# The row of dinv: by way of DRAM instead of by transposes, and the additions of the first graph's outputs one step later, in a two-layer graph kernel

## The chip, the cores and the metric

The kernel runs on one core of a Trainium2 chip, in float32 throughout. The metric is the device time of one launch in microseconds (us); lower is better. The kernel before took 2661.98 us (median of 3 runs, 2660.5 to 2662.49). The profile is of a run of 2660.45 us, and its span from the first to the last instruction is 2658.7 us. Times below that are positions ("at 176.8 us") count from the start of that span.

Engines are named as in the profile: PE is the matrix engine, DVE the vector engine, ACT the scalar engine, POOL the engine that here does the small powers, some additions and issues many of the transfers, SP the one that issues the other transfers. Each engine runs its own instructions in the order in which the program emits them, and waits where an operand or a buffer isn't ready.

## What is computed

There are 16 graphs b of 1024 nodes with 256 features, and one 1024 x 1024 adjacency matrix for all.

```python
# layer 0, for each graph
h = relu(layernorm(x))
g = relu((h.T @ (adj * A_s(h))) * para)         # A_s: from column means of h
q, (k, v) = g.T, h @ kv_w                       # 4 heads of 64
x = x + softmax(q @ k.T * scale) @ v
# layer 1
h = relu(layernorm(x))
A_norm = adj + eye
deg = A_norm.sum(0) + A_norm.sum(1) - diagonal(A_norm)
dinv = rsqrt(deg)
A_hat = A_norm * dinv[:, None] * dinv[None, :]
agg = A_hat @ h
x = x + batchnorm(relu(batchnorm(agg @ W1.T)) @ W2.T)
```

dinv is one vector of 1024 numbers for all graphs. It is used twice: as a factor of each node's row (in the layernorm's scale), and as a factor of each output node of the aggregation. The aggregation is held transposed, with nodes along the columns, so there the kernel needs dinv along the columns, the same in all 128 partitions.

## The kernel before

Node t*128+p lies in partition p. A vector over nodes is a tile of 128 partitions x 8 columns; so is dinv, the last of six such vectors in the tile `deg_sm` (the profile writes `deg`). The row form is the tile `dbc` (128 x 1024; the profile writes `dbc_f`).

**Order.** The program fixes the order of the instructions on each engine by hand (`tc.manual_schedule()`); nothing is moved later. `attention()` (L956) runs over 16 steps for each graph: a *unit* is half of the features and half of the query nodes of a graph, and each of a graph's 4 units has 4 steps. In step s it emits, in this order: the scores of step s on PE with their exponentials on ACT (`scores`, L850, tiles `sc` and `p`), `finish()` of a unit that is due (4 transposes of its output on PE, L934), the first instruction of a piece of background work that asked to be put there (see below), `add_output()` of the unit that was finished (L942 to L952: DVE divides by the sums and adds to x), the sums of exponentials on DVE (`acc`, L885 and L888), the product with the values of step s-1 on PE (`o`, L899), if that was a unit's last step its `sums()` (L916 to L924), and then background work until the step's share of it is done.

**A unit's end.** `sums()` adds the exponentials over the partitions with PE, copies the result to the tile `row` on ACT (L918), and lets POOL send it to DRAM (`sums_d`, L919) and fetch it back across the partitions as `inv` (L924, twice). `add_output()` needs `inv`. A unit that ends in the step s of its `sums()` is put on `pending` with the step s + 2 (L998), and its `finish()` and `add_output()` come in that step.

**Background.** While graph b is in the attention, `background(b)` (L756) prepares graph b+1 or b+2 and, from b = 1 on, does the second layer's aggregation and first product of graph b-1. It is a generator. Each yield gives a cost; the total for a graph is spread over the 16 steps. A yield of `TOP` stops the background for the step, and what follows it is emitted near the top of the next step, before that step's value product.

For b = 0 the background is: queries of graph 1 (`plain_queries`), woven with `graph()` (L230), which forms seven combinations of blocks of the transposed adjacency on POOL and writes them to DRAM (`aht_d`), in 8 pieces of 4 subtractions, 2 loads and 3 stores; and with `degrees()` (L211), which reads the transposed adjacency (tiles `at`), sums it, and ends with dinv. The last step of dinv is `rsqrt` (L79), two POOL instructions (L81, L82). All of `graph()` stands ahead of it in POOL's order. Then come `load_later()` (L276), which loads W1 and allocates `dbc`; a product of keys and values; `columns_of(dinv)` (L183), two DVE copies that spread dinv to two tiles `cb_deg`; another product; and, after a `TOP`, `broadcast_row` (L194): 8 transposes on PE (`cbp_deg`, L199) and 2 copies on ACT to `dbc` (L200). Last comes `prepare(2, products)` (L738), which makes the same kind of row for graph 2 from `csum`: `cb_c` by `columns_of`, then `cbp_c`.

`dbc` is first read in the aggregation of graph 0, in the second graph's attention (L641).

**Buffers that matter.** W1 and `dbc` take the space that `graph()` uses for its adjacency tiles. The pool `py` with the tag `y` has 4 buffers, taken in turn by `two` and `one` of `graph()` (L260, L261; one of each for each piece), by `row` of each unit (L917), and by the `cb` tiles (L187). A new tile waits until the transfer out of the buffer's last tile has landed. The PSUM pool with the tag `mm` has 2 buffers, taken in turn by all products of the background; a product waits until the result two before it has been read. PSUM for the scores has 2 buffers, so that the scores of a step wait for the exponentials of the step before.

Of the kernel before, what the change touches and what calls it, by code (L numbers as in the profile page):

```python
# [10 lines left out]
F32 = mybir.dt.float32  # L11
# [6 lines left out]
P = 128  # L18
# [5 lines left out]
def gnn_two_layers_kernel(  # L24
# [12 lines left out]
    nc = tc.nc  # L37
    B, N, C = x.shape
# [30 lines left out]
    aht_d = dram.tile([7, NP // 2, P, TH, FB], F32, name="aht_d")  # L69
    y1_d = [dram.tile([P, HC, FB], F32, name=f"y1_d{i}") for i in range(B * NH)]  # L70

    sums_d = [dram.tile([2, FB], F32, name=f"sums_d{u}") for u in range(B * CC * NH)]

    UNITS = B * CC * NH
# [9 lines left out]
    def layers(shifted):  # L84
# [60 lines left out]
        def double(slots):  # L145

            for _ in slots:
                next(slots, None)
                yield 0.0
# [58 lines left out]
        later = {}  # L208
# [67 lines left out]
        def load_later():  # L276
            later["w1"] = big.tile([P, CC, H1], F32, tag="w1", name="w1")
            nc.sync.dma_start(out=later["w1"], in_=w1_t.rearrange("(k p) j -> p k j", p=P))
            later["dbc"] = const.tile([P, N], F32, tag="dbc", name=f"dbc_{kind}")

        class Norm:

# [83 lines left out]
        TOP = -1.0  # L366
# [389 lines left out]
        def background(b):  # L756

            if b == 0:
                differences_1 = columns_of(csums[1], "c1")
                yield TOP  # L760
                differences(1, differences_1)
                yield 1.0
                for k in range(CC):
                    yield TOP
                    transposed(1, k)
                    yield 1.0
                w, products, norm = weighers[1], keys_values(1), Norm(2, True).all()
                yield from weave(
                    islice(products, 4), (0, double(islice(w, 8))), (0, islice(norm, 4))
                )  # L770
                yield from weave(
                    plain_queries(1), (0, norm), (0, w), (5, graph()), (7, degrees())
                )
                load_later()
                yield from islice(products, 1)
                cbs = columns_of(dinv, "deg")
                yield from islice(products, 1)
                yield TOP
                broadcast_row(later["dbc"], cbs, "deg")
                yield 1.0  # L780
                yield from prepare(2, products)
                return
            before = hidden(b - 1)
            gather = aggregate(b - 1)
            if b + 1 < B:
                w, products, norm = weighers[b + 1], keys_values(b + 1), normed(b - 1)
                yield from weave(islice(products, 4), (0, islice(w, 4)))
                yield from weave(queries(b + 1), (0, double(w)), (9, islice(norm, 5)))
                yield next(gather)
                yield from weave(products, (0, norm))  # L790
            else:
                yield from weave(endings.pop(), (2, normed(b - 1)))
                yield next(gather)
            if b + 2 < B:
                yield from weave(gather, (7, Norm(b + 2, True).all()))
                yield from prepare(b + 2, before)
            elif b + 2 == B:

                yield from gather
                endings.append(before)  # L800
            else:
                yield from gather
                yield from weave(before, (0, normed_last()))
# [152 lines left out]
        def attention():  # L956

            units = [Unit(b, k, f) for b in range(B) for k in range(CC) for f in range(NH)]
            steps = [(u, g) for u in units for g in range(NG)]
            per_graph = CC * NH * NG  # L960
            before = None
            pending = []
            bg, done, total, top = iter(()), 0.0, 0.0, False
            for s in range(len(steps) + 2):
                if s < len(steps):
                    unit, g = steps[s]
                    b = unit.at[0]
                    if s % per_graph == 0:
                        run(bg)
                        top = False  # L970
                        bg, done = background(b), 0.0
                        total = (37.6 if b > 0 else 41.0) * (b + 1 < B) + 24.0 * (b > 0) + 6.0 * (b + 2 < B)
                        total += 13.7 * (0 < b < B - 2) + 27.4 * (b == B - 1) + 3.0 * (b == 0)

                        total -= 10.3 * (b == B - 1)
                    made = scores(*unit.at, g)
                    due = total * (s % per_graph + 1) / per_graph
                else:
                    due += 5.1
                ended = None  # L980
                if pending and pending[0][1] <= s:
                    ended = pending.pop(0)[0]
                    ended.finish()
                if top:
                    done += advance(bg)
                    top = False
                if ended is not None:
                    ended.add_output()
                if s < len(steps):
                    for pr in made:  # L990
                        unit.add(pr)
                if before is not None:
                    (last, g_last), prs = before
                    last.values(g_last, prs)
                    if g_last == NG - 1:
                        last.sums()

                        pending.append((last, s + (2 if last.index < UNITS - 2 else 1)))  # L998
                while done < due and not top:
                    cost = advance(bg)  # L1000
                    if cost is None:
                        break
                    if cost == TOP:
                        top = True
                        break
                    done += cost
                before = (steps[s], made) if s < len(steps) else None
            run(bg)

        with st:  # L1010
            if shifted:
                for b in range(B):
                    if b > 0:
                        load_x(b)
                    run(Norm(b, True).all())
                    differences(b, columns_of(csums[b], f"c{b}"))
                    for k in range(CC):
                        transposed(b, k)
                    run(islice(weighers[b], AHEAD))
                    run(weave(plain_queries(b), (0, weighers[b])))  # L1020
                    if b == 0:
                        run(degrees(), graph())
                        load_later()
                        broadcast_row(later["dbc"], columns_of(dinv, "deg"), "deg")
                    run(keys_values(b))
                    shifted_attention(b)
                    norm = Norm(b, False)
                    run(norm.all())
                    nc.gpsimd.dma_start(out=x1_d[b], in_=xs[b])
                    if b == B - 1:  # L1030
                        attn.close()
                        turns.append(second(kind))
                    run(aggregate(b), hidden(b))
            else:
                norm = Norm(0, True)
                norm.stats(0, 1)
                norm.scale(0, 2)
                for t in range(2, NT, 2):
                    norm.stats(t, t + 1)
                    norm.shift(t - 2, 2)  # L1040
                    norm.relu(t - 2, t - 1)
                    norm.scale(t, 2)
                norm.shift(NT - 2, 2)
                norm.relu(NT - 2, NT - 1)
                products = keys_values(0)

                for k in range(CC):
                    transposed(0, k, (0,))
                run(islice(products, 2))
                for k in range(CC):  # L1050
                    transposed(0, k, (1,))
                differences(0, columns_of(csums[0], "c0"))
                run(weave(products, (0, islice(weighers[0], AHEAD))))
                load_x(1)
                load_x(2)
                run(weave(plain_queries(0), (0, weighers[0]), (5, Norm(1, True).all())))
                attention()
                attn.close()
                turns.append(second(kind))
                run(aggregate(B - 1), hidden(B - 1))  # L1060
# [324 lines left out]
```

## Time and profile of the kernel before

| Engine | busy, us | share of the span | instructions |
|---|---|---|---|
| PE (matmul) | 2572.0 | 97% | 11882 |
| DVE | 1743.4 | 66% | 2768 |
| ACT | 1336.5 | 50% | 1937 |
| POOL | 564.0 | 21% | 648 |

Transfers moved 355.59 MB, 134 GB/s over the span. The mean granted PE clock was 0.988 of full speed.

Shares over the span say little on a change that touches two of sixteen graphs. The attention of graph 0 lies at about 60 to 206 us, that of graph 1 follows. Views that are read below: the waits of PE (who waited for whom, in us, how often, the longest), the busy time of each engine by stretches of the span, and the timeline (start, duration, engine, line, output <- input, number of instructions merged in the line, and in brackets how long the engine had idled and what ended it). In the timeline DMA_DIRECT2D is the issue of a transfer, not its time.

### The profile page before, as it was taken

The numbers are of one execution on the slowest core, as the hardware profiler recorded it, in microseconds if no ns is written. First come the engines' busy times: TensorE is split into PE (matmuls) and PEld (weight loads), VectorE is DVE, ScalarE is ACT, GpSimd is POOL, SyncE is SP. The second block draws the span as 40 slices with busy tenths as digits, with TensorE's granted clock in tenths as the row PEclk, the third lists the DMA queues.
The fourth block names the chain that finished last, engine by engine and source line by source line (L and its number), as shares of the span: only waits on it lengthen the run. The fifth ranks groups of instructions, "written<-read, shape, count | busy, mean of one in ns | idle before, by whom it ended". The sixth has DMA issues, their size and how long they took to land. (4 is left out here: it accounts for less than half of the span.)

```text
span 2658.7 us, 32181 instructions
## 1 busy us (share of the span) xinstructions
PE 2572.0 (97%) x11882; PEld 951.8 (36%) x11882; DVE 1743.4 (66%) x2768; ACT 1336.5 (50%) x1937; POOL 564.0 (21%) x648
## 2 busy tenths in 40 slices
PE   8959999999999999999999999999999999999995
PEld 3323333333333333333333333333333333334443
DVE  5537576666767675767666676757676675557675
ACT  5635463636454554546373645545463634335544
POOL 1461111111111111111111111111101111026653
PEclk9989999999999999999999999999999999999997
DMA  4451424242423324242424233231524232455559
GB/s 159 145 181 61 166 80 171 84 171 80 143 92 117 122 68 158 68 171 84 171 80 156 87 131 103 93 139 60 174 80 171 80 124 99 135 198 198 198 181 374
DMA packets 131686, 355.59 MB, mean 134 GB/s; under 512 B 17984, under 2 KB 34880, under 8 KB 125376
## 3 DMA queue, kind: packets, MB, share of 16 engines
q1 hardware_dynamic: 104768, 274.25, 29.4%
q0 software_dynamic: 26752, 79.20, 9.0%
q8 instruction: 96, 1.57, 0.2%
q14 instruction: 70, 0.57, 0.1%
HBM read 278.67 MB, written 74.71 MB: 133 GB/s over the span
## 5 line engine op out<-in xcount | busy, mean ns | idle before, releaser
L866 ACT ACTIVATE p<-sc 128x1024 f32<-128x1024 f32 x512 | 495.5, 1019 | 606.3 <-PE sc L858 605.2
L888 DVE TENSOR_TENSOR acc<-acc,p 128x1024 f32<-128x1024 f32 x384 | 471.7, 1228 | 132.0 <-ACT p L866 111.5
L858 PE MATMUL sc<-q,k 64*128 64x512 f32 x2048 | 508.8, 615 | 0.5 <-ACT p L866 0.5
L899 PE MATMUL o<-p,v 128*64 128x512 f32 x2048 | 496.7, 606 | 0.0
L158 PE MATMUL pg<-w,h_a 128*64 128x512 f32 x1600 | 358.1, 592 | 3.4 <-ACT k L595 1.7
L158 PE MATMUL pa<-aht,h_b 128*64 128x512 f32 x1536 | 343.5, 592 | 0.0
L858 PEld LDWEIGHTS sc<-q,k 64*128 64x128 f32 x2048 | 176.1, 186 | 320.4 <-issue 296.8
L919 POOL DMA_DIRECT2D sums_d<-row x64 | 37.5, 586 | 1032.0 <-ACT row L918 1032.0
L158 PE MATMUL py<-at,w 128*64 128x512 f32 x1024 | 230.4, 592 | 0.0
L899 PEld LDWEIGHTS o<-p,v 128*64 128x64 f32 x2048 | 124.5, 136 | 285.4 <-issue 284.7
L408 DVE SCALAR_TENSOR_TENSOR w<-w,adj 128x1024 f32<-128x1024 f32 x128 | 157.2, 1228 | 102.9 <-ACT w L429 99.1
L158 PEld LDWEIGHTS pg<-w,h_a 128*64 128x64 f32 x1600 | 115.5, 137 | 231.8 <-issue 212.8
L158 PEld LDWEIGHTS pa<-aht,h_b 128*64 128x64 f32 x1536 | 110.4, 137 | 213.3 <-issue 197.6
L708 ACT ACTIVATE y<-py,vec 128x512 f32<-128x512 f32 x128 | 87.6, 684 | 168.2 <-PE py L158 111.4
L421 ACT ACTIVATE w<-cbc,csum 128x512 f32<-128x512 f32 x256 | 170.0, 715 | 0.0
L885 DVE TENSOR_TENSOR acc<-p,p 128x1024 f32<-128x1024 f32 x64 | 78.4, 1226 | 109.5 <-ACT p L866 109.5
L709 POOL DMA_DIRECT2D y_d<-y x128 | 70.0, 547 | 316.7 <-ACT y L708 315.6
L429 ACT ACTIVATE w<-w 128x1024 f32<-128x1024 f32 x128 | 134.9, 1054 | 1.8
L483 DVE TENSOR_TENSOR w<-w,w 128x1024 f32<-128x1024 f32 x112 | 132.8, 1216 | 1.8 <-DVE w L408 0.5
L158 PE MATMUL pv<-kvw_f,ht 128*64 128x256 f32 x1024 | 121.0, 384 | 8.8 <-DVE q L575 5.2
L924 POOL DMA_DIRECT2D inv<-sums_d x128 | 98.2, 771 | 145.8 <-DMA sums_d<-row 109.6
L158 PEld LDWEIGHTS py<-at,w 128*64 128x64 f32 x1024 | 74.2, 137 | 145.2 <-issue 128.7
(155 smaller groups left out, 2868.8 us busy)
## 6 DMA issues: line engine op xcount, KB each, us to landing
aht<-aht_d SPq DMA_DIRECT2D x224, 512.0 KB, 6.2
adj<-in_adj_dram SPq DMA_DIRECT2D x128, 512.0 KB, 4.3
y_d<-y POOLq DMA_DIRECT2D x128, 256.0 KB, 2.6
yin_f<-y_d SPq DMA_DIRECT2D x32, 1024.0 KB, 6.3
x<-in_x_dram SPq DMA_DIRECT2D x32, 512.0 KB, 5.0
para<-in_para_dram SPq DMA_DIRECT2D x64, 256.0 KB, 3.9
x_d<-x POOLq DMA_DIRECT2D x16, 1024.0 KB, 10.3
xo_f<-x_d SPq DMA_DIRECT2D x32, 512.0 KB, 8.3
```

The source lines that it names most:

```text
L158: nc.tensor.matmul(dst[r], left[:, r], right, start=start, stop=stop)
L408: nc.vector.scalar_tensor_tensor(w, w, 1.0, a, op0=ALU.add, op1=ALU.mult)
L421: nc.scalar.activation(w[:, t, :], cbc[:, q * FB : (q + 1) * FB], AF.Abs, bias=csum[:, th * TH + t : th * TH + t + 1], scale=-1.0,)
L429: nc.scalar.activation(made[i], made[i], AF.Tanh, scale=-0.5 / C)
L483: nc.vector.tensor_sub(block(i)[part], block(x)[part], block(y)[part])
L708: nc.scalar.activation(y, made, AF.Identity, bias=b1[:, j : j + 1])
L858: nc.tensor.matmul(sc[:, e, :], ks[b][k][r, m * P : (m + 1) * P], qs[b][k][r, f * FB : (f + 1) * FB], start=True, stop=True,)
L866: nc.scalar.activation(pr, sc, AF.Exp)
L885: nc.vector.tensor_add(self.acc, self.held, pr)
L888: nc.vector.tensor_add(self.acc, self.acc, pr)
L899: nc.tensor.matmul(self.o[r, :], vs[b][k][:, m, r], pr[:, e, :], start=(m == 0), stop=(m == NT - 1),)
L924: nc.gpsimd.dma_start(out=self.inv[:, :, e], in_=sums_d[u][e].rearrange("(j q) -> q j", q=P))
```

## The change

dinv no longer goes to `dbc` by DVE copies, PE transposes and ACT copies in the background of graph 0. Instead `load_later()` writes dinv to a DRAM vector of 1024 numbers and reads it back to all partitions, both issued by SP. `load_later()`, the load of W1 with it, moves from the background of graph 0 to that of graph 1, behind the first four products and ahead of the queries of graph 2. This takes the wait for dinv out of DVE's and PE's order.

Separately, the units of graph 0 are finished three steps behind their `sums()` instead of two. This gives the way of the sums through DRAM one more step while POOL is busy with `graph()`.

```diff
+    dinv_d = dram.tile([N], F32, name="dinv_d")
...
             later["dbc"] = const.tile([P, N], F32, tag="dbc", name=f"dbc_{kind}")
+            nc.sync.dma_start(out=dinv_d.rearrange("(t p) -> p t", p=P), in_=dinv)
+            nc.sync.dma_start(
+                out=later["dbc"], in_=dinv_d.rearrange("(o n) -> o n", o=1).to_broadcast([P, N])
+            )
...
-                load_later()
-                yield from islice(products, 1)
-                cbs = columns_of(dinv, "deg")
-                yield from islice(products, 1)
-                yield TOP
-                broadcast_row(later["dbc"], cbs, "deg")
-                yield 1.0
+                yield from islice(products, 2)
                 yield from prepare(2, products)
                 return
...
                 yield from weave(islice(products, 4), (0, islice(w, 4)))
+                if b == 1:
+                    load_later()
                 yield from weave(queries(b + 1), (0, double(w)), (9, islice(norm, 5)))
...
-                        pending.append((last, s + (2 if last.index < UNITS - 2 else 1)))
+
+                        later_by = 3 if last.at[0] == 0 else 2
+                        pending.append((last, s + (later_by if last.index < UNITS - 2 else 1)))
```

A second form of the program, for inputs on which the softmax without a maximum would overflow (L1021 on), gets the same `load_later()`; it isn't run on these inputs.

More of the change, by code (lines that the diff above doesn't have):

```diff
@@ L1023, in layers @@
                         load_later()
-                        broadcast_row(later["dbc"], columns_of(dinv, "deg"), "deg")
                     run(keys_values(b))
```

## The prediction

> **What bounds the kernel now.** I read by stretches first, since 97% for PE hides where the other 3% lie. In each line: the stretch, then busy time of PE, PEld, DVE, ACT, POOL, the granted PE clock, the busy share of the transfer engines, GB/s.
>
> ```profile
> 86.00:163.00 77.00, 70.98 (x326) 24.18 (x326) 44.37 (x67) 49.14 (x78) 51.51 (x64) 0.98 0.59 202
> 163.00:192.00 29.00, 7.39 (x32) 3.38 (x32) 4.55 (x8) 3.60 (x5) 21.06 (x31) 0.65 0.60 204
> 192.00:290.00 98.00, 97.81 (x498) 37.28 (x496) 70.52 (x108) 53.78 (x73) 11.66 (x14) 1.00 0.35 119
> ```
>
> In the last line, the attention that follows, PE is idle for 0.2 us in all, so time is saved only where PE waits. From 163 to 192 it works 7.39 of 29 us. The waits of PE name the cause.
>
> ```profile
> PE cbp_deg L199 <- DVE cb_deg L188: 18.0, 1, 18.0
> ...
> PE pv L158 <- DVE q L575: 5.2, 1, 5.2
> ...
> PE cbp_deg L199 <- DVE v L612: 3.6, 1, 3.6
> ```
>
> Two of these three belong to the transposes that are removed, 21.6 us in sum. That is a ceiling for this part, not its worth: the timeline has to tell what else was late in those us.
>
> ```profile
> 162.97 1.99 PE L858 MATMUL sc<-q,k 64*128 64x512 f32 x8
> ...
> 173.33 0.71 POOL L272 DMA_DIRECT2D aht_d<-two  x1
> ...
> 175.79 0.38 SPq L278 DMA_DIRECT2D w<-in_w_t_dram  x1
> 176.27 1.47 SPq L170 DMA_DIRECT2D adj<-in_adj_dram  x3
> 176.77 0.59 ACT L918 COPY row<-sums 128x512 f32<-128x512 f32 x1 [15.68 <-DMA aht_d<-two]
> 177.25 1.95 ACT L866 ACTIVATE p<-sc 128x1024 f32<-128x1024 f32 x2
> ...
> 179.06 0.71 POOL L272 DMA_DIRECT2D aht_d<-two  x1
> ...
> 180.74 1.67 POOL L82 TENSOR_TENSOR deg<-deg,neg_half 128x8 f32<-128x8 f32 x1
> 182.39 0.64 POOL L919 DMA_DIRECT2D sums_d<-row  x1
> 182.45 0.43 DVE L188 COPY cb_deg<-deg 128x512 f32<-128x512 f32 x1 [21.41 <-POOL deg L82]
> ...
> 186.44 0.43 DVE L188 COPY cb_deg<-deg 128x512 f32<-128x512 f32 x1 [3.57 <-DMA aht_d<-two]
> ...
> 187.68 1.09 PE L199 MATMUL cbp_deg<-ident,cb_deg 128*128 128x128 f32 x4 [3.63 <-DVE v L612]
> 188.70 2.84 PE L899 MATMUL o<-p,v 128*64 128x512 f32 x8
> ...
> 193.19 1.99 PE L858 MATMUL sc<-q,k 64*128 64x512 f32 x8
> ```
>
> Here 162.97 is step 13 of graph 0, 193.19 step 14. Three things are late, all for POOL's sake. (1) ACT has the copy to `row` of the third unit at its head for 15.68 us, with the exponentials of step 13 behind it: `row` takes the buffer of `two` of the last piece but one, issued at 173.33 and landed at 176.77. (2) dinv's power ends at 182.4, behind the last piece of `graph()`. (3) The second `cb_deg` takes the buffer of the last `two`, issued at 179.06 and landed at 186.4: 7.4 us, against 3.4 for the one before. The change removes (2), and (1) and (3) stay.
>
> **What the Trainium skill says.** "DMA: Bandwidth & Descriptors", section "Issuing engines are not separate DMA queues": transfers issued by any engine run on the same 16 engines and interleave. The trace agrees: between 176 and 186 us, with W1 and three adjacency tiles from SP beside POOL's stores, the transfer share is 0.89 and the store in (3) takes twice as long. Same page, "Two DMAs through the same engine are not ordered": a transfer that reads what another wrote must wait for the other's completion. So SP must stand between writing dinv and reading it; the like of it is POOL's wait for `sums_d`, 4.10 and 7.30 us here. Same page, "Rules for kernel authors": where the last dimension isn't contiguous there is one descriptor for each element, so writing dinv is 1024 pieces of 4 bytes. The trace has such a pattern in `inv`: 2 KB in 512 pieces, landing in a median of 2.6 us (2.5 to 5.6). "TensorE: Matmul & The Clock Gate", "What's actually happening": after an idle window of about 3.4 us the clock halves. The trace agrees: clock 0.50 from 176 to 186 us, and the 8 matmuls at 188.70 take 2.84 us instead of 1.94.
>
> **Graph 0, removed.** Two DVE copies (0.43 us each), 8 transposes (1.12 + 1.09 us on PE), two ACT copies (0.59 each), and the `TOP` with its cost of 1.0. The pace of the background is 50/16 = 3.125 for a step. Its sum of costs up to the second product is 3 + 4 x 1.71 + 16 x 1.71 + 2 x 1.71 = 40.62 and step 12 is due 40.625, so step 12 goes on to the next piece: before, the `TOP` of `broadcast_row`; after, `columns_of(csum)` and the third product. Graph 2's own `TOP` then comes in step 14, as before.
>
> **Graph 0, what waits instead.** First the stall of 5.16 us at 153.1: DVE had waited 7.57 us for `inv` of the second unit, until 146.31. With `add_output()` in step 11 (scores at 142.37) instead of step 10 (134.56), DVE does its sums and the product with `para` meanwhile, and PE goes on at about 148. This is hidden at once: PE only comes 5 us sooner to (1). After step 13's scores it now does the value product of step 12 (its exponentials were done at 159.8) and then waits, as step 14's scores need PSUM that ACT frees after `row`: 176.77 + 0.48 + 0.95 = 178.2 us. POOL sets this time, and POOL's order is unchanged: it is busy 12.73 of the 13 us up to 176.
>
> Next (3). The `cb_c` copies of graph 2 now take the two buffers that `cb_deg` took, the second one the last `two`. On DVE the copies of the third product stand behind it, and PE's second half of `cbp_c` needs both. When does that store land? W1 is gone to the next graph, and the adjacency tiles no longer stand behind W1's wait on SP (it waited from 138.8 to 175.8), so they load around 144 to 152, where the transfer share is 0.27. The store then takes about 3.4 to 4 us as its forerunners did, and lands at about 182.7 (182.5 at the earliest by this, 186.4 as before). Then 0.43 (`cb_c`) + 0.75 (two copies of v) gives 183.9, and the half `cbp_c` some 1.1 at the halved clock: the value product of step 13 starts at about 185.0. Before, it started at 196.57. That is 11.6 us. Off this go the 4 transposes of the third unit, which before were done by then and now come in step 15 (0.66), and some 1.5 for the value product and the next product at a clock that rises only now (before, 0.9 of it was paid at 188.70, ahead of the mark). **Gain: 9.4 us.** With the landing at 186.4: 5.7.
>
> The third step's second use: `inv` of the third unit. POOL issues its two transfers after dinv's power, so at about 185.5 (182.39 + 3), and they land near 190. In step 14 DVE would stand 2 to 3 us for it; in step 15 it doesn't. The single PSUM tile for a unit's end is free in time: the next `sums()` come a step later.
>
> **Graph 1, added.** SP issues W1 (0.38 us), the write of dinv, waits for its landing, and issues the read. For the write I take 4 us: `inv` is half its size, so 2.6 to 5.2, and 7.6 is the slowest landing of `sums_d`. For the read, 512 KB like an adjacency tile: 4 us (3.6 to 8.9). Queued behind on SP: `para` of graph 2, issued at 212.35, not used before 237.29 (L469), then an adjacency tile at 217.02, which itself waits for a buffer until then and feeds DVE at 225.46. With the write ending at 212.4 + 4, SP is free before 217; with 7.6 it is 3 us late, still ahead of 225. `dbc` is first read at 290.2, 70 us later. **Cost: 0**, hidden by those slacks and by a transfer share of 0.29 to 0.47 from 207 to 222. The fourth unit's `inv` lands up to 3 us later beside that 1 MB; it has a step of about 9 us more.
>
> The second graph's `normed(0)` asks for the fourth unit only at the tenth piece of the queries, at about 252; step 19 ends before. Cost 0.
>
> **Rivals.** A, the forecast: 2661.98 - 9.4, about **2652.5** (chance 0.58). B, `cb_c` doesn't hold, because stores land sooner or POOL, less disturbed by DVE around 155 to 161 us (its additions there take up to 1.7 us instead of 0.73), ends earlier; then step 14's scores are the mark: 193.19 - 178.2 = 15.0, so 2647 (0.15). Against it speaks that buffers are taken in turn. C, the store lands as late as before: 2661.98 - 5.7 = 2656.3 (0.13). D, the earlier adjacency loads slow POOL's loads, which land 3.4 us after issue and are used 3.4 us after it: 6 pieces by 1 us lengthen everything, 2661.98 - 9.4 + 6 = 2658.6 (0.09). E, slower: C in graph 0, and in graph 1 the write takes 7.6, then the read and the tile behind it 8.9 each: the tile is there at 238 instead of 225, queries of graph 2 wait 13 us, 2656.3 + 13 = 2669 (0.05). Nothing in the trace has such landings at a share under 0.5.
>
> **Numbers.** Faster by over 0.2% (below 2656.7): A, B and 0.08 of C, 0.81. Within: 0.05 of C and D, 0.14. Slower: E, 0.05. The range, 2646.5 to 2657, takes in A to C and leaves out D and E, 0.14.
>
> **What would show it.** Right: no `cbp_deg`; ACT's wait for `row` still ends near 176 to 177; step 14's scores near 178; a shorter stall of PE at `cbp_c`, behind DVE `cb_c` and a landing of `aht_d` near 183; no PE wait from 190 to 300; no DVE wait for `inv` of the second unit over 4 us. Wrong: PE waits in the queries of graph 2, an adjacency tile or `dbc` named as releaser, or POOL's last piece well after 180.

## The result, and the profile after

The changed kernel takes 2648.44 us (median of 4 runs, 2646.87 to 2651.18), the kernel before beside it 2661.24 us (4 runs, 2660.2 to 2662.49). The ratio is 0.9953, with a 95% interval of 0.9936 to 0.9970: 12.8 us less, where 9.4 were forecast; the interval is 8.0 to 17.0 us and holds both. The profiled run is the slowest of the four, 2651.18 us with a span of 2649.3, so its profile shows only 9.4 of the 12.8 us. Some of that was lost before the change acts: the first unit's `sums_d` is issued at 99.90 us instead of 98.64, so positions below lie some 1.3 us later than they would beside the profile of before.

The waits of PE from 86 to 330 us, the changed kernel (releaser, then us in total, times, longest):

```profile
PE sc L859 <- ACT p L867: 13.7, 1, 13.7
PE cbp_c L200 <- DVE v L617: 2.9, 1, 2.9
PE pg L159 <- ACT k L600: 1.7, 2, 0.9
PE pv L159 <- DVE v L617: 0.2, 1, 0.2
```

The 18.0, 5.2 and 3.6 us of before are gone, and 13.7 and 2.9 are new (the 1.7 and 0.2 us stood before too). The sums are 26.8 and 16.6 us, so PE waits 10.2 us less; after the new waits it works at the halved clock for longer, which takes a part back. The stretches of before, read again (busy time of PE, PEld, DVE, ACT, POOL; PE clock; transfer share; GB/s):

```profile
86.00:163.00 77.00, 75.09 (x358) 25.89 (x356) 45.49 (x70) 50.23 (x80) 51.07 (x68) 1.00 0.67 224
163.00:192.00 29.00, 12.58 (x46) 5.42 (x48) 7.92 (x11) 9.26 (x13) 19.51 (x28) 0.65 0.39 131
192.00:290.00 98.00, 97.81 (x484) 35.71 (x480) 69.96 (x106) 49.06 (x66) 11.96 (x14) 1.00 0.43 146
```

PE gains 4.1 us in the first stretch and 5.2 in the second, and nothing in the third, into which the two new transfers went: they cost PE nothing. The second stretch still holds 16.4 us in which PE is idle. The timeline says why:

```profile
158.95 1.99 PE L859 MATMUL sc<-q,k 64*128 64x512 f32 x8
160.87 1.94 PE L900 MATMUL o<-p,v 128*64 128x512 f32 x8
...
171.56 0.71 POOL L273 DMA_DIRECT2D aht_d<-two  x1
...
174.97 0.59 ACT L919 COPY row<-sums 128x512 f32<-128x512 f32 x1 [19.63 <-DMA aht_d<-two]
175.41 0.76 DVE L189 COPY cb_c<-csum 128x512 f32<-128x512 f32 x1 [17.32 <-DMA aht_d<-one]
...
176.54 3.40 PE L859 MATMUL sc<-q,k 64*128 64x512 f32 x8 [13.73 <-ACT p L867]
...
177.47 0.71 POOL L273 DMA_DIRECT2D aht_d<-two  x1
...
182.26 0.43 DVE L189 COPY cb_c<-csum 128x512 f32<-128x512 f32 x1 [6.09 <-DMA aht_d<-two]
...
183.41 1.12 PE L200 MATMUL cbp_c<-ident,cb_c 128*128 128x128 f32 x4 [2.88 <-DVE v L617]
184.45 3.68 PE L900 MATMUL o<-p,v 128*64 128x512 f32 x8
...
190.61 1.99 PE L859 MATMUL sc<-q,k 64*128 64x512 f32 x8
...
196.88 1.99 PE L859 MATMUL sc<-q,k 64*128 64x512 f32 x8
```

Read it against before, step by step. After step 13's scores (158.95) comes the value product at once (160.87), then nothing, since ACT stands at `row` for `two` of the last piece but one. Step 14's scores start at 176.54. The second `cb_c` stands for the last `two` until 182.26, and `cbp_c` behind it. The value product of step 13 starts at 184.45 instead of 196.57, step 15's scores at 190.61 and the first scores of the next graph at 196.88. Before, these two were:

```profile
200.17 1.99 PE L858 MATMUL sc<-q,k 64*128 64x512 f32 x8
...
206.00 1.99 PE L858 MATMUL sc<-q,k 64*128 64x512 f32 x8
```

So 12.1 us are gained at the value product, 9.56 at step 15's scores and 9.12 at the next graph's: nearly the whole gain of this run.

The transfers of dinv, as SP issued them:

```profile
204.45 0.37 SPq L279 DMA_DIRECT2D w<-in_w_t_dram  x1
205.34 0.37 SPq L281 DMA_DIRECT2D dinv_d<-deg  x1
215.97 0.34 SPq L282 DMA_DIRECT2D dbc_f<-dinv_d  x1
216.36 0.43 SPq L468 DMA_DIRECT2D para<-in_para_dram  x1
216.88 0.95 SPq L171 DMA_DIRECT2D adj<-in_adj_dram  x2
```

Between the second and the third line SP stands for the write of 4 KB. It took 10.6 us to land.

### The profile page after: what moved, and what is told of

Read it like the earlier page. It is cut to its first block, busy times and chain, and to the rows that moved or that the text cites. A ratio compares the mean times of both kernels' runs of the same rounds, so it can differ in the third digit from the quotient of the medians.

```text
span 2649.3 us, 32166 instructions
## 1 busy us (share of the span) xinstructions
PE 2571.1 (97%) x11874; PEld 951.7 (36%) x11874; DVE 1741.8 (66%) x2766; ACT 1335.5 (50%) x1935; POOL 561.2 (21%) x648
## 5 line engine op out<-in xcount | busy, mean ns | idle before, releaser
L859 PE MATMUL sc<-q,k 64*128 64x512 f32 x2048 | 510.2, 617 | 14.2 <-ACT p L867 14.2
L717 DVE BATCH_NORM_STATS2 stats<-y 128x6 f32<-128x512 f32 x128 | 85.4, 686 | 59.3 <-ACT y L713 57.4
```

The lines of the kernel that those rows point to most:

```text
L859: nc.tensor.matmul(sc[:, e, :], ks[b][k][r, m * P : (m + 1) * P], qs[b][k][r, f * FB : (f + 1) * FB], start=True, stop=True,)
```

## Experiments

### The two parts, each alone

The changed kernel ran again beside these three variants, as the mark to compare them with.

> The changed kernel again, on the chip of the three runs that take it apart, as their mark. The theory (POOL's graph() sets the end of the stall, by the buffers that row and cb_c take over from it) and the rivals expect the same of it: about 2648.5 us, 0.9950 of the kernel before.

It took 2648.80 us (5 runs, 2646.66 to 2649.91), 0.9951 of before (0.9938 to 0.9965).

The first part alone:

```diff
-                        later_by = 3 if last.at[0] == 0 else 2
+                        later_by = 2
```

> Only the first part: dinv by way of DRAM in graph 1; outputs of graph 0 added two steps behind, as before. Theory: the 5.2 us stall at 153 us comes back, but PE only reaches the wait for row 5 us later, and that wait ends with POOL as before. In step 14 DVE then stands some 1 to 3 us for the third unit's inv. So 2649 to 2652 us, 10 to 12 us less than before. Rival (the third step brings its own 5.2 us): 2653.5 us or more.

2653.23 us (6 runs, 2652.55 to 2658.16), 0.9973 (0.9961 to 0.9985). That is close to the rival's number (2653.5 or more) and above the theory's range: without the third step 4.4 us are lost. The waits of PE, from 86 to 330 us:

```profile
PE sc L859 <- ACT p L867: 11.7, 1, 11.7
PE pv L159 <- DVE q L580: 4.6, 1, 4.6
PE cbp_c L200 <- DVE v L617: 2.2, 1, 2.2
```

The wait of about 5 us is back, and the one behind `row` is shorter, as the theory had it. But it is shorter by 2 us (11.7, and 13.4 in the mark) and not by 5: `row` itself came later, at 178.45 us instead of 174.34 in the mark.

The second part alone, on the kernel before:

```diff
-                        pending.append((last, s + (2 if last.index < UNITS - 2 else 1)))
+                        later_by = 3 if last.at[0] == 0 else 2
+                        pending.append((last, s + (later_by if last.index < UNITS - 2 else 1)))
```

> Only the second part: outputs of graph 0 added three steps behind; dinv by copies and transposes in graph 0, as before. Theory: the stall at 153 us goes, and PE stands that much longer for cb_deg, which ends with POOL: 2659 to 2662 us, no change. Rival (the parts add up): 2655.5 to 2657 us.

2655.05 us (10 runs, 2653.82 to 2655.47), 0.9977 (0.9967 to 0.9986): 6.2 us less than before, again close to the rival's range. The waits of PE:

```profile
PE cbp_deg L199 <- DVE cb_deg L188: 18.5, 1, 18.5
PE cbp_deg L199 <- DVE v L612: 3.5, 1, 3.5
```

The wait for `cb_deg` is no longer than before (18.0), although PE came 6 us sooner to it (step 13's scores at 156.30 instead of 162.97). So what it waits for came 6 us sooner too: the first `cb_deg` at 176.27 instead of 182.45. The theory's sentence on the first part, "that wait ends with POOL as before", was wrong in the last two words.

The parts alone give 8.0 and 6.2 us, 14.2 in sum; both together give 12.4, so they nearly add up.

### Where POOL gained its time

POOL's time for `graph()`, from the issue of its first load behind the first unit's `inv` to the end of the issue of its last store, read from each timeline, and the same for its first three pieces:

| Kernel | first three pieces, us | all, us |
|---|---|---|
| before | 32.8 | 78.1 |
| first part alone | 33.3 | 79.8 |
| second part alone | 28.5 | 71.6 |
| changed | 28.5 | 74.9 to 75.2 |

Each kernel with three steps gains 4.3 to 4.8 us in the first three pieces, from 102 to 135 us, before the second unit's wait for `inv` at all. Only the first unit's `add_output()` falls there. In the kernel before (DVE and POOL in the timeline):

```profile
109.30 0.81 DVE L949 TENSOR_TENSOR x<-os,x 128x512 f32<-128x512 f32 x1
...
110.17 3.29 DVE L888 TENSOR_TENSOR acc<-acc,p 128x1024 f32<-128x1024 f32 x2
110.97 1.40 POOL L268 TENSOR_TENSOR au_f<-au_f 128x256 f32<-128x256 f32 x1
112.33 1.71 POOL L269 TENSOR_TENSOR one<-au_f,two 128x256 f32<-128x256 f32 x1
...
116.00 2.90 DVE L888 TENSOR_TENSOR acc<-acc,p 128x1024 f32<-128x1024 f32 x2
116.07 1.75 POOL L264 TENSOR_TENSOR two<-au_f 128x256 f32<-128x256 f32 x1
117.90 1.59 POOL L265 TENSOR_TENSOR two<-au_f,two 128x256 f32<-128x256 f32 x1
...
126.34 0.46 POOL L259 TENSOR_TENSOR au_f<-au_f,ident 128x128 f32<-128x128 f32 x1 [1.51 <-DMA au_f<-in_adj_t_dram]
...
129.99 1.46 POOL L245 DMA_DIRECT2D au_f<-in_adj_t_dram  x2 [1.70 <-DMA aht_d<-au_f]
```

A subtraction of 128 x 256 takes POOL 0.73 us when DVE is still and 1.4 to 1.75 us beside DVE's additions. The Trainium skill says this in "SBUF — State Buffer", section "Who interferes with whom": a DVE instruction with two inputs in SBUF contends with a GpSimd instruction that reads SBUF; the trace agrees. (It isn't always POOL that pays: at 120.49 a small product of DVE, usually 0.29 us, took 2.00 beside two subtractions of 0.73.) Four subtractions are slowed here, and then POOL waits twice for its own transfers, 3.2 us. Two kernels ask which unit's third step does it. Only the first unit three steps behind:

```diff
-                        later_by = 3 if last.at[0] == 0 else 2
+                        later_by = 3 if last.index == 0 else 2
```

> The changed kernel, but only the first unit of graph 0 is added three steps behind; the other three are added two behind, as before. New theory (the third step pays through POOL: the first unit's additions on DVE no longer fall on the first pieces of graph(), and POOL forms its first three pieces in 28.5 us instead of 33): nearly the whole of the third step's 4.4 us stays, 2648.5 to 2650.5 us, with PE's 5 us wait at the second unit back and hidden. Rival (it pays through the second unit's wait for inv on DVE): as with two steps for all, 2653 us.

2648.78 us (5 runs, 2645.79 to 2649.21), 0.9952 (0.9939 to 0.9966) of before on another chip: all of it. The profile is of its fastest run, 2645.79 us. In its timeline the same subtractions read:

```profile
108.59 3.31 DVE L889 TENSOR_TENSOR acc<-acc,p 128x1024 f32<-128x1024 f32 x2 [0.45 <-ACT p L867]
109.22 1.60 POOL L266 TENSOR_TENSOR two<-au_f,two 128x256 f32<-128x256 f32 x1
...
112.23 0.74 POOL L269 TENSOR_TENSOR au_f<-au_f 128x256 f32<-128x256 f32 x1
112.92 0.74 POOL L270 TENSOR_TENSOR one<-au_f,two 128x256 f32<-128x256 f32 x1
...
115.68 0.74 POOL L265 TENSOR_TENSOR two<-au_f 128x256 f32<-128x256 f32 x1
...
116.50 0.74 POOL L266 TENSOR_TENSOR two<-au_f,two 128x256 f32<-128x256 f32 x1
```

DVE's sums now come 1.6 us sooner, because the reciprocal, the product and the addition that stood ahead of them are gone to the next step, and they fall in part on POOL's issue of loads (110.76 to 112.2). The first unit's addition isn't gone from these pieces: it comes at 116.91 instead of 109.30. Two subtractions are still slow (109.22 and 119.61) instead of four. The two waits for transfers are gone; the first three pieces take 28.5 us. PE's 5 us at the second unit, which were expected back, are down to 0.7: POOL issues the second unit's `inv` at 137.04 instead of 142.86.

Only the second unit three steps behind:

```diff
-                        later_by = 3 if last.at[0] == 0 else 2
+                        later_by = 3 if last.index == 1 else 2
```

> The changed kernel, but only the second unit of graph 0 is added three steps behind; the others two. New theory: POOL's first three pieces take 33 us again, and although PE's 5 us wait at the second unit is gone, the wait for row ends as late as with two steps for all: 2652 to 2654 us. Rival: the 4.4 us stay, 2648.5 to 2649.5 us.

2652.30 us (6 runs, 2650.25 to 2654.92, the same chip as the one before), 0.9967 (0.9955 to 0.9979), with 32.7 us for the first three pieces. PE's wait at the second unit is gone and one of 14.4 us stands behind `row`. The medians of the two runs lie 3.5 us apart, as the new theory has it. That it is the first unit's delay that counts is shown; that POOL's two waits for transfers go because its subtractions and loads no longer come late is read from the timeline and wasn't isolated. A rival stands untested: with the first unit delayed, SP's loads of the tiles `at` begin later (122.42 us instead of 120.60) and POOL's load of the third piece is issued sooner (117.35 instead of 119.44), so that the two may hinder each other less.

### Where W1 is loaded

```diff
+        def load_w1():
+            later["w1"] = big.tile([P, CC, H1], F32, tag="w1", name="w1")
+            nc.sync.dma_start(out=later["w1"], in_=w1_t.rearrange("(k p) j -> p k j", p=P))
...
         def load_later():
-            later["w1"] = big.tile([P, CC, H1], F32, tag="w1", name="w1")
-            nc.sync.dma_start(out=later["w1"], in_=w1_t.rearrange("(k p) j -> p k j", p=P))
...
+                load_w1()
                 yield from islice(products, 2)
```

> The changed kernel, but W1 is loaded in graph 0 where it was before, and only dinv's two transfers are in graph 1. Theory (the load of W1 and the adjacency tiles held behind it on SP crowd POOL's last store, on whose buffer the second cb_c stands): that store lands 6 to 8 us after its issue instead of 4.8, cb_c comes 2 to 4 us later, 2650.5 to 2652.5 us. Rival (where W1 is loaded does not matter; the gain is the removed transposes alone): 2648.5 us.

2649.62 us (5 runs, 2649.17 to 2651.17), 0.9958 (0.9945 to 0.9972). The time can't be told from the mark's, and both theories miss half of it:

```profile
172.70 0.71 POOL L273 DMA_DIRECT2D aht_d<-two  x1
...
180.84 0.43 DVE L189 COPY cb_c<-csum 128x512 f32<-128x512 f32 x1 [9.43 <-DMA aht_d<-two]
```

The last store landed 8.1 us after its issue, as expected with the crowd behind W1 (5.0 in the mark: 176.80 to 181.81). But it was issued 4 us sooner, as `graph()` took 71.3 us instead of 74.9. With W1 at its head, SP holds back graph 2's adjacency tiles until 169 us; without it they load from 143 us on, beside POOL's loads. Between these two profiles, moving W1 costs POOL some 3.5 us and saves 3.1 at the last landing. That the earlier tiles are what slows POOL isn't shown: in the two runs with only one unit delayed, W1 was moved too, and POOL took 43.4 and 43.2 us for the last five pieces, against 42.8 in this run and 46.4 to 46.8 in the changed kernel.

### Taking POOL's holds away one by one

The third unit's `row` gets the idle buffer of the tile `db`:

```diff
-                row = py.tile([P, FB], F32, tag="y", name=f"row_{self.name}")
+                pool, tag = (p1, "s1") if u == 2 else (py, "y")
+                row = pool.tile([P, FB], F32, tag=tag, name=f"row_{self.name}")
```

> The changed kernel, but row of the third unit takes a buffer of its own (that of the tile db, idle by then) instead of one of graph()'s. Theory: ACT no longer stands for POOL's store, step 14's scores come near 161 us instead of 176.5, and the next hold is cb_c, which then takes the buffers of the last piece but one of graph(), landed at about 175; behind it add_output of the third unit stands for inv until about 187. 3 to 6 us less than the changed kernel, not 13.7: 2643 to 2646 us. Rival (the wait for row is the whole stall): 14 us less, 2635 us.

2644.73 us (5 runs, 2642.78 to 2645.22), 0.9938 (0.9925 to 0.9952). The longest wait of PE from 86 to 330 us is now this one:

```profile
PE cbp_c L200 <- DVE cb_c L189: 9.3, 1, 9.3
```

Step 14's scores come at 162.88, 13.7 us sooner than in the changed kernel's profile, and 4 us are left of it at the end, as expected. Then the `cb_c` pair too leaves the four buffers:

```diff
+            if name == "c2":
+                both = p3.tile([P, NT // 4, 4, P], F32, tag="ht", name=f"cb_{name}")
             for g in range(NT // 4):
-                cb = py.tile([P, 4, P], F32, tag="y", name=f"cb_{name}_{g}")
+                if name == "c2":
+                    cb = both[:, g]
+                else:
+                    cb = py.tile([P, 4, P], F32, tag="y", name=f"cb_{name}_{g}")
```

> As the one before, and the two cb_c tiles take a buffer that graph() does not use (that of an ht tile). Theory: now the third unit's inv is the next hold: POOL issues its transfers after graph() and dinv, so they land near 187 us, DVE stands at add_output in step 15 from about 170, and the rest of that step and the next stands behind DVE. Again only 3 to 6 us less than the changed kernel: 2642 to 2646 us. Rival (buffers alone are the cause): 16 us less or more, 2632 us.

2643.99 us (5 runs, 2641.39 to 2645.3), 0.9935 (0.9922 to 0.9949): nothing that can be told from the one before. The hold moved on to `inv`, which POOL sends for behind `graph()` and dinv. In the timeline of this run:

```profile
181.98 0.64 POOL L926 DMA_DIRECT2D sums_d<-row  x1
183.92 1.54 POOL L931 DMA_DIRECT2D inv<-sums_d  x2 [1.30 <-DMA sums_d<-row]
187.36 0.20 DVE L949 RECIPROCAL inv<-inv 128x8 f32<-128x8 f32 x1 [14.14 <-DMA inv<-sums_d]
...
191.67 1.98 PE L922 MATMUL sums<-acc,ones 128*64 128x512 f32 x4 [12.66 <-DVE acc L894]
```

Last, the third unit's sums go by SP:

```diff
+                issue = nc.sync if u == 2 else nc.gpsimd
-                nc.gpsimd.dma_start(
+                issue.dma_start(
                     out=sums_d[u], in_=row.rearrange("(e r) c -> e r c", r=HD)[:, 0, :]
...
-                    nc.gpsimd.dma_start(
+                    issue.dma_start(
                         out=self.inv[:, :, e], in_=sums_d[u][e].rearrange("(j q) -> q j", q=P)
```

> As the one before, and the third unit's sums go to DRAM and back by SP instead of POOL. Theory: nothing in the attention of graph 0 stands behind POOL's graph() any more; the 13.7 + 2.9 us of stall and some 2 to 3 us at the halved clock go: 2629 to 2633 us. Rival (another wait, of DVE or of transfers crowded by graph(), takes over half or more of it): 2638 us or more.

2631.03 us (4 runs, 2630.24 to 2631.39), 0.9888 of before (0.9873 to 0.9903): 17.8 us less than the changed kernel, 29.8 less than before. The same stretch as above, in this run:

```profile
163.00:192.00 29.00, 28.28 (x146) 11.28 (x144) 21.13 (x25) 22.20 (x31) 18.40 (x21) 1.00 0.70 232
```

PE is idle for 0.7 of 29 us and its clock never drops. POOL's `graph()` takes 80.1 us here, longer than in any other run, and PE doesn't wait for it. This version beats both kernels. The three holds were taken away in this order only; `inv` or `cb_c` alone wasn't tried.

### The slow write

`load_later()` keeps W1; the two transfers of dinv follow the queries of graph 2:

```diff
                 yield from weave(queries(b + 1), (0, double(w)), (9, islice(norm, 5)))
+                if b == 1:
+                    send_dinv()
```

> The changed kernel, but dinv is written to DRAM and read back behind the queries of graph 2, where hardly anything else is transferred. In the changed kernel the write of 1024 pieces of 4 bytes landed 10.6 us after its issue, beside W1 and two adjacency tiles. If the pieces are the cost, it still takes 8 us or more; if the crowd was, it takes 3 to 5 us. The time is the same in both, about 2648.5 us, as long as dbc is there before the first aggregation ends its second product.

One run, 2651.36 us, too few to compare its time. The write landed 11.1 us after its issue, so the crowd of W1 and adjacency tiles isn't the cause. The place wasn't as quiet as meant: POOL's store of x (1 MB) ran beside it. And here the write cost PE a wait. The aggregation's first loads stand behind it on SP (L635 in the timeline), and PE waits for them:

```profile
251.25 0.39 SPq L283 DMA_DIRECT2D dinv_d<-deg  x1
262.45 0.33 SPq L284 DMA_DIRECT2D dbc_f<-dinv_d  x1
262.87 3.94 SPq L635 DMA_DIRECT2D aht<-aht_d  x5
```

```profile
PE pa L159 <- DMA aht<-aht_d: 3.6, 1, 3.6
```

## Why the prediction was right, and where it was off

**The main chain held.** The ceiling of 21.6 us was not the worth; `row`, then `cb_c` on the last `two`, took over, as worked out. The marks: step 14's scores 178.2 forecast, 176.54 measured; landing of the last store 182.7 and about 182.2; value product of step 13 at 185.0 and 184.45; the gain behind the third unit's transposes 9.4 us and 9.12. Inside this, two sizes were off and cancelled: the value product came 12.1 us sooner, not 11.6, and the halved clock took back 2.6 us up to step 15's scores, not 1.5. The median, 12.8 us less, lies nearer to rival B's number (2647) than to the forecast, but B's first mechanism didn't come: `cb_c` did hold PE, for 2.9 us. The experiments show the order of the holds: with `row` alone away 4.1 us come, with `cb_c` too nothing more that can be told, and only with `inv` away the 17.8.

**The step that was mis-sized** is "This is hidden at once", and under it "POOL sets this time, and POOL's order is unchanged". The third step was priced at 0 there, and at 2 to 3 us saved from a wait of DVE. It is worth 4.4 us with the first part and 6.2 without it. POOL's order is unchanged, but not its pace: with the first unit's output added nearly 8 us later on DVE, the first pieces of `graph()` gained 4.3 us. Rival B had named this cause ("less disturbed by DVE"), at the wrong place, around 155 to 161 us, and gave it 0.15. That DVE would stand 2 to 3 us for the third unit's `inv` in step 14 was too much: 0.5 us with two steps (at 189.97 in the run of the first part alone).

**Left open.** Rival D, the earlier adjacency tiles slowing POOL, may be half true: 3.5 us of pace, not 6, between the changed kernel and the one with W1 early, but two other runs with W1 moved don't show it. The last landing took 4.8 us, not the 3.4 to 4 that were read from its forerunners; their median in the kernel before was 4.2. (The share of 0.27 that the prediction gives for 144 to 152 us is that of 142 to 152; the shorter stretch has 0.30.) In the profiled run what POOL gained in its first pieces was nearly cancelled by a slower rest and this landing, so that the marks fit better than the reasons did. That is luck.

**Hidden as forecast, for another size.** The write of dinv was put at 4 us, with 7.6 as the slowest; it takes 9.6 to 11.3 us in the ten traces that have it. SP was free at 216.0, the adjacency tiles behind it still fed DVE in time, and PE was idle for 0.2 us from 192 to 290, as before. The slack that was read, up to 225, covered the miss. The fourth unit's `inv` was put at up to 3 us later; it landed 10.8 us after its issue instead of 3.5, and DVE, three steps behind, didn't wait for it.

## What to carry to other kernels

A wait that is removed is worth the distance to the next thing that is late for the same cause. Here three consumers stood behind one engine, two by shared buffers and one by its queue, and 17.8 us came only when all three were taken away. "Its order is unchanged" doesn't mean that an engine ends at the same time: look for two engines that slow each other before a delay elsewhere is called hidden. In a queue that works in order, the wait for a small transfer to land can be longer than for a large one (here 10.6 us for the 4 KB of dinv, 4.7 for the 512 KB of W1), so it belongs where nothing urgent stands behind it.

## What the runs showed of the hardware

Writing 4 KB to DRAM as 1024 pieces of 4 bytes took 9.6 to 11.3 us to land, in ten traces and beside quite different neighbours. `sums_d`, 4 KB as two pieces of 2 KB, landed in 1.6 us just before (issued at 202.56 in the changed kernel), and W1, 512 KB, in 4.7. That the pieces are the cause fits all of these, but a write of fewer pieces of the same data wasn't tried. Other transfers aren't what it stands for in the end: in the changed kernel the profile shows no transfer at work in the last 6 us before it landed (the stretch view again, transfer share 0.00):

```profile
210.00:216.00 6.00, 6.00 (x30) 1.96 (x28) 5.33 (x6) 4.11 (x6) 0.00 (x0) 1.00 0.00 0
```

Small transfers of another queue land late beside it. `inv`, issued at 204.5 and 205.3, landed after 10.8 us; with the write moved away but W1 still beside it (the run above), it took 6.0, and its median over the kernel before is 2.6. So some 4.8 of the 8.2 us of delay are the write's, by one trace without it. In the version with all holds away, POOL sent the fourth unit's `sums_d` at 185.15, when SP issued the write at 185.20; both landed at about 196.1, and POOL stood for it:

```profile
196.36 1.54 POOL L932 DMA_DIRECT2D inv<-sums_d  x2 [10.57 <-DMA sums_d<-row]
```
